# Involution kernel: matrices evicted in runs of three elements, and full-width matmuls in place of 32-column tiles

## The chip, the cores and the metric

The kernel runs on one core of a Trainium2 chip. The metric is the device time of one execution in microseconds (us); lower is better. The engines are named as in the profile: PE is TensorE (PEld its weight loads), DVE is VectorE, ACT is ScalarE, POOL is GpSimd and SP is SyncE, which here only issues DMAs.

## What is computed

The input is x, 8 x 256 x 56 x 56, float32. Two residual layers follow each other, each on a group-normalised copy of x:

```python
x = x + involution(gn(x))          # layer 0
x = x + tri_conv_block(gn(x))      # layer 1: two 3x3 convolutions with ternary weights, batch norms, ReLUs

def involution(x):                 # 7x7, 16 groups of 16 channels
    ker = einsum('bchw,oc->bohw', x, w_reduce) + b_reduce     # 256 -> 64 channels
    ker = einsum('bchw,oc->bohw', ker, w_span) + b_span       # 64 -> 49 * 16
    patches = [padded x shifted by (i, j) for i in range(7) for j in range(7)]
    return (ker.reshape(B, 16, 1, 49, H, W) * patches.reshape(B, 16, 16, 49, H, W)).sum(axis=3)
```

Every pixel has its own 7 x 7 kernel for each of the 16 groups. Only layer 0 is touched by the change.

## The kernel before

The program has three stages: the involution (`ph1`), the two convolutions (`ph2`, `ph3`, matmuls on line 202) and a last pass that combines and stores. The involution takes roughly the first half of the time.

**Tiling of the involution.** A tile is 3 x 8 pixels (`PY` x `PX`, `NP` = 24). There are 19 rows of 7 tiles (`TY`, `TX`, together `NT` = 133). The 9 x 14 neighbourhood of a tile has `NQ` = 126 positions. For one tile and one group the involution is a matrix product: the neighbourhood's pixels (126 positions by channels) against a matrix of 126 positions by 24 output pixels that holds the kernels at the places where they apply. The work goes over 16 chunks: 8 batches, and in each two halves `t` of 128 channels (8 groups).

**`prep(b)`** is a generator with ten steps, one for each strip of six image rows. POOL normalises the strip (`xn`, L304), PE reduces it to 64 channels twice over (`pk`, L310), ACT adds the bias and writes it sorted by pixel within the tile (`kr`, L323). PE also transposes the strip (`pt`, L328), ACT copies it to `stg` (L333), and a DMA on ACT's queue stores it in `xt_d` (L336; `xtd` in the profile), a padded copy in DRAM with pixels first and channels inside, one row being `WQ` pixels. There are two such copies, used by even and odd batches in turn. The strips for batch b+1 are prepared while the second half of batch b is applied.

**`generate(b, t, a)`** makes the matrices of a chunk, `a`, in 32 units. A unit is three pixels and two groups: six float32 matmuls of 64 rows, 126 columns and 133 tiles, each of which shows as two instructions (`pg`, L373). The two groups use the two halves of the PE rows and write to two banks of one PSUM tile. The eviction adds the span bias and writes to `a`, whose rows hold, for each tile, 8 groups x 24 pixels: three units of four are evicted by one DVE instruction (L385), the fourth by six ACT instructions (L381). On DVE the innermost run goes over the 133 tiles, so that one element follows another at a step of 192 elements.

**`apply_rows(b, t, a, q, i)`** applies two rows of tiles (one in the last of ten groups). For every tile there are four matmuls, one for each pair of groups, each with 32 channels as stationary columns and 48 moving columns, on the four 32-column parts of PE (`pa`, L398). The result has, for each channel, the values of both groups of its pair. One ACT instruction copies the even group's values times 1 or 0 (L406), one DVE instruction for each row adds the odd group's times 0 or 1 (L408), and POOL adds the sum to x in place (L413).

**`load_q`** fetches the neighbourhoods `q` of a group of two rows from `xt_d`: nine DMAs a row, of 14 partitions each, on the SP queue (L359). `qpool` has three buffers, and `prefetch` keeps up to three groups under way across chunks. PSUM is one pool of four tiles of two banks (`ps_tile`), shared by all of these.

**The order** is that of the loop at the end of the function: for each chunk, `generate`, then ten times apply, prefetch and one `prep` step, then the group-norm statistics of the result and its store (`x1d`). A scheduler places the instructions on the queues and sets the semaphores; each engine takes its queue in order.

Of the kernel before, what the change touches and what calls it, by code (L numbers as in the profile page):

```python
# [7 lines left out]
F32 = mybir.dt.float32  # L8
F32R = mybir.dt.float32r
AF = mybir.ActivationFunctionType  # L10
ALU = mybir.AluOpType
# [4 lines left out]
P = 128  # L16
B, C, H, W = 8, 256, 56, 56
HW = H * W
CT = C // P
K, PAD, G = 7, 3, 16  # L20
KK = K * K
GT = G // CT
GP = GT // 2
# [4 lines left out]
PY, PX = 3, 8  # L28
TY, TX = 19, W // PX
NT = TY * TX  # L30
NP = PY * PX
QY, QX = PY + K - 1, PX + K - 1
NQ = QY * QX
LEAD = (PY - 1) * QX + PX - 1
WL = LEAD + NQ
HQ, WQ = TY * PY + K - 1, 64
SR = 6
NS = -(-H // SR)
QG = 2
NQG = -(-TY // QG)  # L40
NX = PY * W
# [10 lines left out]
def involution_tri_block_kernel(  # L52
# [3 lines left out]
    nc = tc.nc  # L56
    x = x.rearrange("b c h w -> b c (h w)")
# [189 lines left out]
    with ExitStack() as ph1:  # L247
        ps_p = ph1.enter_context(tc.tile_pool(name="ps_p", bufs=4, space=PSUM))

        def ps_tile(name):  # L250
            return ps_p.tile([P, 2, 512], F32, tag="ps", name=name)
# [6 lines left out]
        work = ph1.enter_context(tc.tile_pool(name="work", bufs=2))  # L258
# [11 lines left out]
        xs = {(0, t): load_x(0, t) for t in range(CT)}  # L270
# [8 lines left out]
        half_sb = fixed([P, 2], "half_sb", half)  # L279
# [6 lines left out]
        wl = fixed([P, CT, GP, WL], "wl", w_line)  # L286
# [11 lines left out]
        def prep(b, pr):  # L298

            for s in range(NS):  # L300
                n = min(SR, H - s * SR)
                strip = xn[s % 2]
                for t in range(CT):
                    nc.gpsimd.tensor_scalar(  # L304
                        strip[:, t, :n, PAD:PAD + W],
                        xs[b, t][:, s * SR * W:(s * SR + n) * W].rearrange("p (h w) -> p h w", w=W),
                        pr[t][:, 0:1], pr[t][:, 1:2], ALU.mult, ALU.add)
                pk = ps_flat(f"pk_{b}_{s}")
                for t in range(CT):
                    nc.tensor.matmul(pk[:, :n * W], wr[:, t, :], strip[:, t, :n, PAD:PAD + W],  # L310
                                     start=(t == 0), stop=(t == CT - 1))
                ty = s * SR // PY
                for y in range(min(PY, n)):
                    m = -(-(n - y) // PY)
                    rows = pk[:, y * W:y * W + W]
                    if m == 2:
                        rows = pk[:, :n * W].rearrange("p (a f) -> p a f", f=NX)[:, :, y * W:y * W + W]
                        src = rows.rearrange("p a (t x) -> p a t x", x=PX)
                        dst = kr[:, y, :, ty:ty + m, :].rearrange("p x a t -> p a t x")
                    else:  # L320
                        src = rows.rearrange("p (t x) -> p t x", x=PX)
                        dst = kr[:, y, :, ty, :].rearrange("p x t -> p t x")
                    nc.scalar.activation(dst, src, AF.Identity, bias=br)  # L323
                nb = n // 2
                pt = ps_flat(f"pt_{b}_{s}")
                for k in range(nb):
                    for t in range(CT):
                        nc.tensor.transpose(  # L328
                            pt[:2 * WQ, k * C + t * P:k * C + (t + 1) * P],
                            strip[:, t, 2 * k:2 * k + 2, :].rearrange("p r w -> p (r w)"),  # L330
                            ident_sb)
                stg = work.tile([P, SR // 2, C], F32, tag="stg", bufs=3, name=f"stg_{b}_{s}")
                nc.scalar.copy(stg[:2 * WQ, :nb, :].rearrange("p k c -> p (k c)"),  # L333
                               pt[:2 * WQ, :nb * C])
                o = (PAD + s * SR) * WQ
                nc.scalar.dma_start(  # L336
                    xt_d[b % 2][o:o + n * WQ, :].rearrange("(k p) c -> p k c", p=2 * WQ),
                    stg[:2 * WQ, :nb, :])
                yield
# [22 lines left out]
        def generate(b, t, a):  # L362

            av = a[:NQ].rearrange("q t (g p) -> q g p t", g=GT)
            for u in range(GP * NP // 3):
                gp, p0 = u // (NP // 3), u % (NP // 3) * 3
                ps = ps_tile(f"pg_{b}_{t}_{u}")
                for j in range(3):
                    py, px = (p0 + j) // PX, (p0 + j) % PX
                    o = LEAD - py * QX - px  # L370
                    for h in range(2):
                        rows = slice(h * CR, (h + 1) * CR)
                        nc.tensor.matmul(  # L373
                            ps[:NQ, h, j * NT:(j + 1) * NT], wl[rows, t, gp, o:o + NQ],
                            kr[rows, py, px].rearrange("r a t -> r (a t)"),
                            start=True, stop=True)
                g0 = 2 * gp
                if u % 4 == 3:
                    for h in range(2):
                        for j in range(3):  # L380
                            nc.scalar.activation(  # L381
                                av[:, g0 + h, p0 + j], ps[:NQ, h, j * NT:(j + 1) * NT],
                                AF.Identity, bias=bt[:, t, g0 + h, p0 + j:p0 + j + 1])
                else:
                    nc.vector.tensor_tensor(  # L385
                        av[:, g0:g0 + 2, p0:p0 + 3],
                        ps[:NQ, :, :3 * NT].rearrange("q h (p t) -> q h p t", t=NT),
                        bt[:, t, g0:g0 + 2, p0:p0 + 3].unsqueeze(3).to_broadcast([NQ, 2, 3, NT]),
                        ALU.add)

        def apply_rows(b, t, a, q, i):

            ty, n = i * QG, min(QG, TY - i * QG)
            ps = ps_tile(f"pa_{b}_{t}_{i}")
            for r in range(n):
                for k in range(TX):
                    for g in range(GP):
                        nc.tensor.matmul(  # L398
                            ps[g * 32:(g + 1) * 32, r, k * 2 * NP:(k + 1) * 2 * NP],
                            q[:NQ, r, k, g * 32:(g + 1) * 32],  # L400
                            a[:NQ, (ty + r) * TX + k, g * 2 * NP:(g + 1) * 2 * NP],
                            start=True, stop=True)
            even, odd = (ps[:, :n, :TX * 2 * NP].rearrange("c r (k h p) -> c r k h p", k=TX, h=2)
                         [:, :, :, h].rearrange("c r k p -> c r k p") for h in range(2))
            inv = work.tile([P, QG, TX, NP], F32, tag="inv", bufs=3, name=f"inv_{b}_{t}_{i}")
            nc.scalar.activation(inv[:, :n], even, AF.Copy, scale=half_sb[:, 0:1])  # L406
            for r in range(n):
                nc.vector.scalar_tensor_tensor(inv[:, r], odd[:, r], half_sb[:, 1:2], inv[:, r],  # L408
                                               ALU.mult, ALU.add)
                m = min(PY, H - (ty + r) * PY)  # L410
                xv = xs[b, t][:, (ty + r) * NX:(ty + r) * NX + m * W]
                xv = xv.rearrange("p (y t x) -> p y t x", t=TX, x=PX)
                nc.gpsimd.tensor_tensor(  # L413
                    xv, xv, inv[:, r].rearrange("p t (y x) -> p y t x", y=PY)[:, :m], ALU.add)

        chunks = [(b, t) for b in range(B) for t in range(CT)]
        queue = [(b, t, i) for b, t in chunks for i in range(NQG)]
# [2 lines left out]
        def prefetch(upto):  # L420
            while queue and len(loads) < upto:
                k = queue.pop(0)
                loads[k] = load_q(*k)

        nprm = [None] * CT
        for b, t in chunks:
            more = b + 1 < B
            if t == 0:
                prefetch(3)
                if more:  # L430
                    xs[b + 1, 0] = load_x(b + 1, 0)
            a = apool.tile([P, NT, GT * NP], F32, tag="a", name=f"a_{b}_{t}")
            generate(b, t, a)
            steps = iter(())
            if t == 1 and more:
                xs[b + 1, 1] = load_x(b + 1, 1)
                nprm[1] = params(b + 1, 1, xs[b + 1, 1])
                steps = prep(b + 1, list(nprm))
            for i in range(NQG):
                apply_rows(b, t, a, loads.pop((b, t, i)), i)  # L440
                if t == 0 or i + 3 < NQG:
                    prefetch(3)
                if i == 4 and t == 0 and more:
                    nprm[0] = params(b + 1, 0, xs[b + 1, 0])
                next(steps, None)
            for _ in steps:
                pass
            group_norm_params(xs[b, t], ps_flat, gn2[:, b, t, :], f"b{b}{t}")
            nc.sync.dma_start(x1_d[b][t], xs[b, t])
# [131 lines left out]
```

## Time and profile before

| | |
|---|---|
| Median of 3 runs | 3955.49 us (3952.43 to 3955.94) |
| Profiled execution | 3955.94 us, its span 3954.2 us |
| PE busy, PEld busy | 2750.0 us (70%), 2414.5 us (61%) |
| DVE, ACT, POOL busy | 1253.3 us (32%), 848.0 us (21%), 302.5 us (8%) |
| DMA | 431.79 MB, 387086 packets |
| Mean granted TensorE clock | 0.825 |

Busy times are shares of the whole span and hide that the stages have different limits; so the involution has to be read by stretches. In a group line the number after x is how often the instruction ran, then come the total busy time in us and the mean of one in ns, then the idle time of the engine just before them and what ended it. The granted clock of PE is given as a share of full speed. A line of the chain in time gives the start in us, the length in us and the engine or DMA that held the end up.

### The profile page before, as it was taken

How to read it: one execution, taken by the hardware profiler on the slowest of the kernel's cores; microseconds unless marked ns; L12 is line 12 of the kernel's file. 1: busy time of each engine (PE TensorE's matmuls, PEld its weight loads, DVE VectorE, ACT ScalarE, POOL GpSimd, SP SyncE). 2: the span in 40 equal slices, each digit the busy share in tenths (PEclk: the TensorE clock that was granted, in tenths of full speed). 3: DMA queues.
4: the chain of work that ended last, by engine and by line, in shares of the span. 5: the costliest groups of instructions: out<-in, count | busy, mean ns of one | idle time of the engine just before them, and what ended most of it. 6: DMA issues, size and time to landing. Idle time of an engine off the chain costs nothing.

```text
span 3954.2 us, 73934 instructions
## 1 busy us (share of the span) xinstructions
PE 2750.0 (70%) x32132; PEld 2414.5 (61%) x32132; DVE 1253.3 (32%) x1675; ACT 848.0 (21%) x1595; POOL 302.5 (8%) x491
## 2 busy tenths in 40 slices
PE   3455565556545455554399999999799999999500
PEld 2444544445444445444288888888688888888400
DVE  5445534254452444534331111110111111110254
ACT  2122221222212122221031111110121111110243
POOL 1111111201002110110300000000200000000000
PEclk8677776667767787776599999999899999999755
DMA  5233343333334333333431111100221111100499
GB/s 182 76 120 119 120 126 115 101 117 121 116 113 124 109 118 118 122 112 105 144 128 63 63 63 63 63 31 31 79 81 63 63 63 63 63 31 0 173 406 396
DMA packets 387086, 431.79 MB, mean 109 GB/s; under 512 B 46576, under 2 KB 369742, under 8 KB 369870
## 3 DMA queue, kind: packets, MB, share of 16 engines
q1 hardware_dynamic: 350496, 360.54, 27.0%
q10 hardware_dynamic: 36268, 66.53, 4.6%
q8 instruction: 256, 4.19, 0.5%
q14 instruction: 66, 0.52, 0.0%
HBM read 295.56 MB, written 131.33 MB: 108 GB/s over the span
## 4 chain that ended last, share of the span: by engine, by line
PE 50%; DVE 17%; SPq 15%; DMA 13%; issue 3%; ACT 2%; POOL 0%; ACTq 0%; DVEq 0%; POOLq 0%
PE c L202 43%; SPq L359 15%; DVE a L385 13%; DMA xtd<-stg 3%; DMA q<-xtd 3%; PE pa L398 3%; PE pk L310 3%; DMA x1f<-x1d 2%; DMA y1f<-y1d 1%; PE pt L328 1%; ACT stg L333 1%; DVE x1f L522 1%; DMA out_y<-x1f 1%; DVE st_a L113 1%; DMA y2f<-y2d 1%
## 5 line engine op out<-in xcount | busy, mean ns | idle before, releaser
L202 PE MATMUL c<-o,wq 128*128 128x448 f32 x8064 | 1704.3, 374 | 35.2 <-ACT o L192 31.9
L202 PEld LDWEIGHTS c<-o,wq 128*128 128x128 f32 x8064 | 1525.1, 189 | 214.1 <-ACT o L192 32.4
L398 PE MATMUL pa<-a,q 126*32 126x48 f32 x17024 | 351.2, 254 | 671.8 <-DMA q<-xtd 630.3
L398 PEld LDWEIGHTS pa<-a,q 126*32 126x32 f32 x17024 | 307.3, 145 | 718.0 <-issue 497.2
L385 DVE TENSOR_TENSOR a<-pg,bt 126x798 f32<-126x798 f32 x384 | 528.3, 1524 | 7.6 <-DMA wqd<-wq_w 7.0
L373 PE MATMUL pg<-kr,wl 64*126 64x133 f32 x6144 | 442.6, 296 | 98.0 <-DVE a L385 97.3
L373 PEld LDWEIGHTS pg<-kr,wl 64*126 64x126 f32 x6144 | 399.3, 199 | 138.3 <-DVE a L385 137.5
L408 DVE SCALAR_TENSOR_TENSOR inv<-pa,half_sb,inv 128x168 f32<-128x168 f32 x304 | 105.9, 388 | 916.3 <-ACT inv L406 916.3
L381 ACT ACTIVATE a<-pg,bt 126x133 f32<-126x133 f32 x768 | 230.4, 479 | 328.7 <-PE pg L373 307.3
L465 DVE BATCH_NORM_STATS2 st<-y 128x6 f32<-128x448 f32 x112 | 70.2, 627 | 681.4 <-ACT y L464 681.4
L413 POOL TENSOR_TENSOR x<-x,inv 128x168 f32<-128x168 f32 (+1 forms) x304 | 155.5, 531 | 1026.0 <-DVE inv L408 1025.9
L406 ACT ACTIVATE inv<-pa,half_sb 128x336 f32<-128x336 f32 (+1 forms) x160 | 84.2, 526 | 610.9 <-PE pa L398 572.8
L464 ACT COPY y<-c 128x448 f32<-128x448 f32 x112 | 59.5, 532 | 663.3 <-PE c L202 663.3
L498 DVE BATCH_NORM_STATS2 st<-y 128x6 f32<-128x448 f32 x84 | 52.5, 626 | 460.9 <-ACT y L497 460.9
L310 PE MATMUL pk<-xn,wr 128*128 128x336 f32 (+1 forms) x320 | 159.7, 641 | 24.6 <-POOL xn L304 24.6
L323 ACT ACTIVATE kr<-pk,br 128x112 f32<-128x112 f32 (+1 forms) x232 | 74.6, 453 | 381.2 <-PE pk L310 380.4
L497 ACT COPY y<-c 128x448 f32<-128x448 f32 x84 | 44.7, 532 | 475.2 <-PE c L202 475.2
L304 POOL TENSOR_SCALAR xn<-x,gn 128x336 f32<-128x336 f32 (+1 forms) x160 | 95.6, 607 | 661.9 <-DVE gn L129 362.8
L310 PEld LDWEIGHTS pk<-xn,wr 128*128 128x128 f32 x320 | 77.9, 276 | 57.1 <-POOL xn L304 25.4
L221 POOL MEMSET o<- 128x3364 f32 x16 | 45.6, 2902 | 850.4 <-PE c L202 850.3
L328 PEld LDWEIGHTS pt<-ident_sb,xn 128*128 128x128 f32 x448 | 73.3, 181 | 29.1 <-issue 21.0
L113 DVE BATCH_NORM_STATS2 st_b<-x 128x6 f32<-128x448 f32 x112 | 69.8, 623 | 66.9 <-POOL x L413 66.9
(93 smaller groups left out, 965.2 us busy)
## 6 DMA issues: line engine op xcount, KB each, us to landing
q<-xtd SPq DMA_DIRECT2D x2736, 49.0 KB
xtd<-stg ACTq DMA_DIRECT2D x72, 384.0 KB
x<-in_x SPq DMA_DIRECT2D x16, 1568.0 KB
x1d<-x SPq DMA_DIRECT2D x16, 1568.0 KB
x1l<-x1d SPq DMA_DIRECT2D x16, 1568.0 KB
y1d<-y SPq DMA_DIRECT2D x112, 224.0 KB
y1l<-y1d SPq DMA_DIRECT2D x16, 1568.0 KB
y1f<-y1d SPq DMA_DIRECT2D x16, 1568.0 KB
```

The costliest lines, as they stand in the source:

```text
L113: nc.vector.bn_stats(st[:, j, :], xt[:, j * NC:(j + 1) * NC])
L202: nc.tensor.matmul(ps[:, :NC], wq[:, t, tap, t_out * P:(t_out + 1) * P], part[t][:, j * CRW + dy:j * CRW + dy + CRW, dx:dx + W], start=(n ...
L304: nc.gpsimd.tensor_scalar(strip[:, t, :n, PAD:PAD + W], xs[b, t][:, s * SR * W:(s * SR + n) * W].rearrange("p (h w) -> p h w", w=W), pr[t] ...
L310: nc.tensor.matmul(pk[:, :n * W], wr[:, t, :], strip[:, t, :n, PAD:PAD + W], start=(t == 0), stop=(t == CT - 1))
L328: nc.tensor.transpose(pt[:2 * WQ, k * C + t * P:k * C + (t + 1) * P], strip[:, t, 2 * k:2 * k + 2, :].rearrange("p r w -> p (r w)"), ident_sb)
L359: nc.sync.dma_start(q[qy * QX:(qy + 1) * QX, r], src)
L373: nc.tensor.matmul(ps[:NQ, h, j * NT:(j + 1) * NT], wl[rows, t, gp, o:o + NQ], kr[rows, py, px].rearrange("r a t -> r (a t)"), start=True, ...
L381: nc.scalar.activation(av[:, g0 + h, p0 + j], ps[:NQ, h, j * NT:(j + 1) * NT], AF.Identity, bias=bt[:, t, g0 + h, p0 + j:p0 + j + 1])
L385: nc.vector.tensor_tensor(av[:, g0:g0 + 2, p0:p0 + 3], ps[:NQ, :, :3 * NT].rearrange("q h (p t) -> q h p t", t=NT), bt[:, t, g0:g0 + 2, p0 ...
L398: nc.tensor.matmul(ps[g * 32:(g + 1) * 32, r, k * 2 * NP:(k + 1) * 2 * NP], q[:NQ, r, k, g * 32:(g + 1) * 32], a[:NQ, (ty + r) * TX + k, g ...
L408: nc.vector.scalar_tensor_tensor(inv[:, r], odd[:, r], half_sb[:, 1:2], inv[:, r], ALU.mult, ALU.add)
L413: nc.gpsimd.tensor_tensor(xv, xv, inv[:, r].rearrange("p t (y x) -> p y t x", y=PY)[:, :m], ALU.add)
```

## The change

The change has five parts.

1. In `generate`, the matmuls of the units that DVE evicts write every third column of their PSUM bank, so that the three pixels of a unit lie side by side for each tile. The DVE instruction then goes over tiles outside and pixels inside and writes three neighbouring elements at a time. ACT's units are as before.
2. `apply_rows` becomes `apply_row`. One row of tiles is applied at a time, with one matmul of 128 stationary columns and 192 moving columns for each tile, in two PSUM tiles of four and three image tiles. Each output channel then has the values of all eight groups, and for each 32 partitions one ACT and one DVE instruction pick the two groups that belong there: eight ACT and eight DVE instructions a row, on 32 partitions each. The POOL addition is as before.
3. A row of `xt_d` has 62 pixels in place of 64, so that a transposed pair of image rows has 124 partitions in place of 128, and the pad-row stores have 62.
4. The store from `stg` to `xt_d` is issued by SP in place of ACT, and `stg` has two buffers in place of three.
5. The loop goes over 19 rows in place of ten groups; prefetch still follows every second row, and `prep` still takes ten steps in a chunk.

```diff
-HQ, WQ = TY * PY + K - 1, 64
+HQ, WQ = TY * PY + K - 1, W + K - 1
...
-                stg = work.tile([P, SR // 2, C], F32, tag="stg", bufs=3, name=f"stg_{b}_{s}")
+                stg = work.tile([P, SR // 2, C], F32, tag="stg", name=f"stg_{b}_{s}")
...
-                nc.scalar.dma_start(
+                nc.sync.dma_start(
                     xt_d[b % 2][o:o + n * WQ, :].rearrange("(k p) c -> p k c", p=2 * WQ),
                     stg[:2 * WQ, :nb, :])
...
+                on_act = u % 4 == 3
...
+                        if on_act:
+                            dst = ps[:NQ, h, j * NT:(j + 1) * NT]
+                        else:
+                            dst = ps[:NQ, h, j:3 * NT:3]
                         nc.tensor.matmul(
-                            ps[:NQ, h, j * NT:(j + 1) * NT], wl[rows, t, gp, o:o + NQ],
+                            dst, wl[rows, t, gp, o:o + NQ],
...
                     nc.vector.tensor_tensor(
-                        av[:, g0:g0 + 2, p0:p0 + 3],
-                        ps[:NQ, :, :3 * NT].rearrange("q h (p t) -> q h p t", t=NT),
-                        bt[:, t, g0:g0 + 2, p0:p0 + 3].unsqueeze(3).to_broadcast([NQ, 2, 3, NT]),
+                        av[:, g0:g0 + 2, p0:p0 + 3].rearrange("q g p t -> q g t p"),
+                        ps[:NQ, :, :3 * NT].rearrange("q h (t p) -> q h t p", p=3),
+                        bt[:, t, g0:g0 + 2, p0:p0 + 3].unsqueeze(2).to_broadcast([NQ, 2, NT, 3]),
                         ALU.add)
...
-        def apply_rows(b, t, a, q, i):
...
+        def apply_row(b, t, a, q, ty):
+            inv = work.tile([P, TX, NP], F32, tag="inv", bufs=3, name=f"inv_{b}_{t}_{ty}")
+            for t0, n in ((0, 4), (4, 3)):
+                ps = ps_tile(f"pa_{b}_{t}_{ty}_{t0}").rearrange("p a (k f) -> p (a k) f", k=2)
+                for i in range(n):
+                    nc.tensor.matmul(ps[:, i, :GT * NP], q[:NQ, ty % QG, t0 + i, :],
+                                     a[:NQ, ty * TX + t0 + i, :], start=True, stop=True)
+                for j in range(4):
+                    rows = slice(j * 32, (j + 1) * 32)
+                    dst = inv[rows, t0:t0 + n, :]
+                    even, odd = (ps[rows, :n, g * NP:(g + 1) * NP] for g in (2 * j, 2 * j + 1))
+                    nc.scalar.activation(dst, even, AF.Copy, scale=half_sb[rows, 0:1])
+                    nc.vector.scalar_tensor_tensor(dst, odd, half_sb[rows, 1:2], dst,
+                                                   ALU.mult, ALU.add)
...
-            for i in range(NQG):
-                apply_rows(b, t, a, loads.pop((b, t, i)), i)
-                if t == 0 or i + 3 < NQG:
-                    prefetch(3)
-                if i == 4 and t == 0 and more:
+            for ty in range(TY):
+                i = ty // QG
+                apply_row(b, t, a, loads[b, t, i], ty)
+                if ty % QG == QG - 1 or ty == TY - 1:
+                    del loads[b, t, i]
+                    if t == 0 or i + 3 < NQG:
+                        prefetch(3)
+                if ty == 8 and t == 0 and more:
                     nprm[0] = params(b + 1, 0, xs[b + 1, 0])
-                next(steps, None)
+                if ty % 2 == 1 or ty > 16:
+                    next(steps, None)
```

More of the change, by code (lines that the diff above doesn't have):

```diff
@@ L377, in generate @@
                 g0 = 2 * gp
-                if u % 4 == 3:
+                if on_act:
                     for h in range(2):
@@ L389, in generate @@
                         ALU.add)
-        def apply_rows(b, t, a, q, i):
[L393 to L414, printed above, removed]
@@ new lines, in apply_row @@
+        def apply_row(b, t, a, q, ty):
[12 more added lines that the diff above has]
+                                                   ALU.mult, ALU.add)
+            n = min(PY, H - ty * PY)
+            xv = xs[b, t][:, ty * NX:ty * NX + n * W].rearrange("p (y t x) -> p y t x", t=TX, x=PX)
+            nc.gpsimd.tensor_tensor(
+                xv, xv, inv.rearrange("p t (y x) -> p y t x", y=PY)[:, :n], ALU.add)
```

## The prediction

> **What bounds the kernel now.** I read the page's forty slices first, then the groups, then stretches of one batch, then the SyncE queue's own waits and the chain in time. The slices split the span in two: up to about 1960 us PE is half busy at a changing clock (the involution stage), after that PE shows 9 (the convolutions) and the end is DMA. The diff touches only the first part. Its groups:
>
> ```profile
> L385 DVE TENSOR_TENSOR a<-pg,bt 126x798 f32<-126x798 f32 x384 | 528.3, 1524 | 7.6 <-DMA wqd<-wq_w 7.0
> L373 PE MATMUL pg<-kr,wl 64*126 64x133 f32 x6144 | 442.6, 296 | 98.0 <-DVE a L385 97.3
> L398 PE MATMUL pa<-a,q 126*32 126x48 f32 x17024 | 351.2, 254 | 671.8 <-DMA q<-xtd 630.3
> L408 DVE SCALAR_TENSOR_TENSOR inv<-pa,half_sb,inv 128x168 f32<-128x168 f32 x304 | 105.9, 388 | 916.3 <-ACT inv L406 916.3
> L381 ACT ACTIVATE a<-pg,bt 126x133 f32<-126x133 f32 x768 | 230.4, 479 | 328.7 <-PE pg L373 307.3
> ```
>
> In `generate` DVE never waits (7.6 us in all) and PE waits for DVE; in the apply stage PE waits for the `q` loads. Busy time by stretch: a generate, an apply of a first channel half (t=0), an apply of a second half with `prep` of the next batch in it (t=1):
>
> ```profile
> core 0: us, PE busy (x) PEld busy (x) DVE busy (x) ACT busy (x) POOL busy (x), PEclk, DMA share, GB/s
> 325.00:358.00 33.00, 26.63 (x388) 23.64 (x384) 32.93 (x28) 14.42 (x48) 0.00 (x0) 0.96 0.44 133
> 358.60:421.00 62.40, 21.36 (x1000) 18.75 (x1000) 15.49 (x44) 5.06 (x10) 10.53 (x20) 0.58 0.35 98
> 468.00:559.00 91.00, 50.55 (x1162) 38.63 (x1162) 12.11 (x35) 21.32 (x50) 20.42 (x37) 0.67 0.36 108
> ```
>
> Generate: 24 DVE evictions fill 33.0 us, 1.374 us each. What PE alone needs shows where it runs unhindered, in the same table for `pg` alone:
>
> ```profile
> 327.50:328.90 1.40, 1.40 (x28) 1.40 (x28) 1.40 (x2) 0.43 (x2) 1.00 0.18 44
> ```
>
> 28 matmul instructions in 1.40 us; their records start in pairs 110 ns apart at full clock, so a unit (12 instructions) takes 0.66 us and 32 units 21.1 us. Apply at t=0 is SyncE issuing: 122 `q` DMAs 0.436 us apart, with seven long ones, 62 us. Apply at t=1 is a loop, seen in the SyncE queue's waits and in the chain in time:
>
> ```profile
> SPq L359 <- PE pa L398: 262.1, 16, 28.5
> SPq L359 <- DMA xtd<-stg: 240.0, 64, 12.4
> ```
> ```profile
> 499.10 2.52 DMA xtd<-stg
> 501.64 0.31 SPq L359
> ...
> 503.73 1.88 DMA q<-xtd
> 505.61 1.33 PE pa L398 x56
> 506.94 2.54 PE pk L310 x4
> 509.48 1.29 PE pt L328 x6
> 510.80 0.81 ACT stg L333
> 511.62 2.53 DMA xtd<-stg
> ```
>
> The records show eight DMA semaphores used in turn over both queues, so a `q` load waits until the DMA eight places before it has landed; when that is the `stg` store, the loop turns once in 12.5 us.
>
> **What the Trainium skill says.** (1) "SBUF — State Buffer", Specifications (TRN2): two hits on a 16-byte line are needed for full bandwidth. The trace agrees that scattered writes cost: DVE's contiguous rows (168 elements 388 ns, 3136 elements 3428 ns) give 216 ns + 1.02 ns each, so 798 would take 1033 ns, and L385, writing single elements 768 bytes apart, takes 1524. (2) "PSUM — Partial Sum Buffer", Specifications (TRN2): any non-contiguous pattern slows matmuls significantly, without a figure. No matmul here writes a stepped output. (3) "DMA: Bandwidth & Descriptors", Why a DMA increments its semaphore by 16 and not by 1: a DMA is spread over the largest number of engines up to 16 that divides the slowest dimension. The packet records agree: the 126-row load of `bt` never has more than 14 packets in flight, the 128-row `stg` store 16 and more. (4) "PSUM — Partial Sum Buffer", PSUM bank collisions: two engines must not touch one bank in the same 32 partitions together; other quadrants may. No run here shows it.
>
> **The change, part by part.**
>
> *Generate.* DVE writes runs of three. At 12-byte runs, two of three DVE units start so that one element of each run stands alone on a 16-byte line: 798 x 2/3 x 1/3 = 177 elements, at the scattered surcharge (1524-1033)/798 = 0.62 ns, 0.11 us. So 1033+110 = 1143 ns; consecutive evictions overlap 150 ns today (1524-1374), giving 0.99 us, 23.8 us for 24. PE's 21.1 us and ACT's 14.4 lie below. With the two now so close and four PSUM buffers I take 26: **-7 us** a generate, 16 times, -112. Bounds: 21.2 us of DVE with no lone element (-10 us); no gain at all if the run length is not what costs. PE's stepped write is the unknown: between nothing and twice the time for the three units of four that use it. I take nothing: a convolution instruction writes 448 columns in 211 ns (1704.3 us over 8064), 0.47 ns a column, while a `pg` instruction needs 110 ns for 133, 0.83 ns each, so the write side should have slack. That is an inference, and the first rival is its failure.
>
> *Apply, t=0.* 17024 32-column matmuls go, 4256 of 192 columns come. `pk` instructions of 336 columns start 0.56 us apart at a clock of 0.5, so 192 columns take 0.32 there and 0.16 at a clock of 1.0: a row (14) 2.2 to 4.5 us against 1.35. SyncE needs 4.6 us a row (18 x 0.436 + 1.2 of long ones, halved) and covers it, except for the two ends of a chunk: the first group is released later (+1.8) and the last row comes later (+1.8). ACT: 8 small activations a row; contiguous ACT rows (540 ns for 336, 400 for 168) give 260 + 0.83 each, 340 and 320 ns, overlapping to some 0.15; 1.2 us a row. DVE: 8 at 216 + 1.02 each, 314 and 290 ns, 1.75 us a row overlapped. Both hide under 4.6; only the last half row shows, +0.4. **+4 us** a chunk; nine chunks without `prep` (+36).
>
> *Apply, t=1.* The `stg` store goes to SyncE and has 124 rows. 124 divides by 4, so four engines carry 93 packets of 1 KB each; such packets take 47 ns here, so 4.4 us instead of 1.3, landing 5.7 us after issue instead of 2.5 (estimate from the skill's rule). Behind the store stand the `q` loads: seven go on in 3.5 us, the eighth waits 2.2. The store itself should not wait for ACT: it is written after a load that SyncE needs 9 us to issue. So a group is 9.0 + 0.4 + 2.2 = 11.6 us against 12.5, seven times: -6. Against that: +4 at the ends as above, and with two `stg` buffers the copy of the last strips waits for a store of 5.7 us, with the evictions behind it on ACT, +4. **+2 us**, seven times (+14). Bounds: 10 to 13 us a group, -10 to +11.
>
> *Start.* The 14 pad-row stores have 62 rows, so two engines at 31 x 46 ns: 20 us in sequence on ACT's queue, where they now take 12, with the `w1` loads behind them; batch 0's ten stores take 4.4 us each where the strips follow each other in 2.1 now. This lies beside the weight reduction but not wholly. **+20** (10 to 30).
>
> *Nothing:* fewer transposed rows and smaller pads, hidden on PE and POOL; the POOL adds keep their number.
>
> Sum: -112 + 36 + 14 + 20 = -42. The profiled execution took 3955.94 us (span 3954.2), the median of three 3955.49, so 3914 either way.
>
> **Rivals.**
>
> *PE becomes the bound of generate* (slower). If the stepped write halves PE's pace, a pair takes 220 ns: 24 units of 1.32 and 8 of 0.66 make 37.0 us, +4 a generate, 64 + 70 = +134, 4090. It decides from 1.5 times on: 24 x 0.99 + 5.3 = 29 us leaves -4, which the other 70 eat. For it: the skill's sentence. Against: the slower stream. Between them, at 1.4 times, -72 + 70: 3954.
>
> *Runs of three do not help DVE* (the change doesn't do what it says): only the +70 remains, 4026. For it: no DVE row here has such runs. Against: `kr` written by ACT (532-byte steps, 460 ns for 112 elements) is as dear as `a`, and contiguous rows are not.
>
> *The small evictions become the bound.* If the four quadrants of a bank are read one after another by ACT and DVE in turn, a row is 8 steps of ACT, DVE and two hand-overs of 35 ns, 4 x 0.72 + 4 x 0.69 = 5.6 us, above SyncE's 4.6, and nothing runs ahead: 107 us for 19 rows at t=0 (+45), about the same at t=1 with `prep`'s 2.2 us a group on ACT. 16 x 41 on top of the sum: near 4570. Against: the two half rows lie in different banks and can alternate.
>
> **How the numbers follow.** Main case 0.42, with its own range 3850 to 3960; PE at 1.4 times 0.13; PE at twice 0.23; DVE not helped 0.10; evictions 0.12. I call no change what lies within 0.2%, 8 us. Faster: 0.33 of the main case and 0.05 of the middle one, 0.38; same 0.08; slower 0.54, though no single slower case is as likely as the main one. The range 3840 to 4110 leaves out the eviction case and a few hundredths at either end.
>
> **What would show it.** Right: L385 near 1140 ns; generate 24 to 27 us; matmul pairs of `pg` at 110 ns; t=0 apply 65 to 67 us with SyncE issuing throughout; `xtd<-stg` landing after more than 5 us and SyncE waiting about 2 us behind it. Wrong: pairs of 150 ns or more; L385 above 1400; PE waiting for ACT or DVE instead of `q`, or SyncE standing long before a store whose copy is not done.

## The result and the profile after

The changed kernel takes **4091.48 us** (median, 4089.27 to 4096.95) against 3954.76 us for the kernel before on the same chip: a ratio of 1.0349, 95% interval 1.0331 to 1.0366. It is slower by 3.5%; the forecast was 3914 us, and the time lies near the upper end of its range. The profiled execution has a span of 4087.1 us. Its groups on the page answer to those shown of before:

```profile
L402 PE MATMUL pa<-a,q 126*128 126x192 f32 x4256 | 877.1, 367 | 295.5 <-issue 126.3
L409 DVE SCALAR_TENSOR_TENSOR inv<-pa,half_sb,inv 32x72 f32<-32x72 f32 (+1 forms) x2432 | 732.6, 301 | 572.6 <-ACT inv L408 482.9
L408 ACT ACTIVATE inv<-pa,half_sb 32x72 f32<-32x72 f32 (+1 forms) x2432 | 784.6, 323 | 423.1 <-DVE inv L409 265.9
L379 PE MATMUL pg<-kr,wl 64*126 64x133 f32 x6144 | 404.0, 293 | 21.6 <-DVE a L391 20.0
L391 DVE TENSOR_TENSOR a<-pg,bt 126x798 f32<-126x798 f32 x384 | 370.6, 1042 | 22.5 <-PE pg L379 14.2
```

The `generate` eviction fell from 1524 to 1042 ns, and PE's wait for it from 97.3 to 20.0 us. In the apply stage PE waited for `q` before; now ACT and DVE name each other as the engine that ends most of their idle time. The stretches that answer to the three of before are a generate, an apply at t=0 and an apply at t=1:

```profile
core 0: us, PE busy (x) PEld busy (x) DVE busy (x) ACT busy (x) POOL busy (x), PEclk, DMA share, GB/s
613.20:637.80 24.60, 22.77 (x372) 22.20 (x368) 23.04 (x25) 14.42 (x48) 0.00 (x0) 0.97 0.39 111
637.80:713.30 75.50, 54.84 (x270) 50.53 (x270) 51.88 (x166) 45.60 (x143) 10.40 (x19) 0.89 0.40 119
754.60:857.00 102.40, 73.07 (x358) 62.92 (x358) 48.50 (x159) 63.26 (x180) 20.43 (x36) 0.90 0.31 85
```

Generate went from 33.0 to 24.6 us, the t=0 apply from 62.4 to 75.5. The wait that sets the end of a t=0 row can be read from the chain in time there:

```profile
694.77 0.34 ACT inv L408
695.11 0.03 issue
695.13 0.32 DVE inv L409
695.47 0.34 ACT inv L408
695.82 0.03 issue
695.84 0.32 DVE inv L409
696.19 0.34 ACT inv L408
696.53 0.03 issue
696.55 0.33 DVE inv L409
```

ACT and DVE take turns, 0.71 us for a pair, although the two engines work on different 32 partitions and only the DVE instruction needs the ACT one of its own 32 partitions (a quadrant). The two half rows alternate on both engines: while DVE has a quadrant of one, ACT has a quadrant of the other. So a row takes five such pairs, 3.5 us, and not eight. At t=1 the same chain passes through the store (the length on the DMA line is from issue to landing):

```profile
812.15 0.39 SPq L359
812.54 0.05 issue
812.63 8.71 DMA xtd<-stg
821.46 0.78 issue
822.24 0.34 ACT inv L408
```

What waits for the store there is ACT's next copy to `stg`, because one of the two buffers has to come free; the line of the page has such waits at 131.0 us in all:

```profile
L333 ACT COPY stg<-pt 124x768 f32<-124x768 f32 x80 | 61.4, 768 | 132.2 <-DMA xtd<-stg 131.0
```

Adding up the two traces by stage, with the stage's borders at the first eviction of `generate` on DVE and its last on either engine, the next chunk's first eviction, and the first convolution matmul:

| stage | before, us | after, us | change | forecast |
|---|---|---|---|---|
| start, to the first `generate` eviction on DVE | 90.0 | 109.8 | +19.8 | +20 |
| 16 generates | 528.9 | 402.1 | -126.8 | -112 |
| 8 applies at t=0, to the next generate | 559.6 | 678.1 | +118.5 | +32 |
| last apply (no `prep`), to the first convolution | 96.6 | 104.2 | +7.6 | +4 |
| 7 applies at t=1 with `prep`, to the next generate | 709.0 | 823.6 | +114.6 | +14 |
| sum: first convolution matmul | 1984.0 | 2117.8 | +133.8 | -42 |

After the first convolution the two are alike (1970.2 and 1969.3 us to the end of the span).

### The profile page after: what moved, and what is told of

Its sections match the earlier page's. It is cut to its first block, busy times and chain, and to the rows that moved or that the text cites. A ratio compares the mean times of both kernels' runs of the same rounds, so it can differ in the third digit from the quotient of the medians.

```text
span 4087.1 us, 53613 instructions
## 1 busy us (share of the span) xinstructions
PE 3178.9 (78%) x19364; PEld 2862.7 (70%) x19364; DVE 1726.1 (42%) x3803; ACT 1566.2 (38%) x3867; POOL 306.4 (7%) x491
## 4 chain that ended last, share of the span: by engine, by line
PE 54%; DVE 14%; DMA 14%; ACT 10%; issue 4%; SPq 3%; POOL 1%; ACTq 1%; DVEq 0%; POOLq 0%
PE c L202 42%; DMA xtd<-stg 8%; ACT inv L408 7%; DVE inv L409 7%; PE pg L379 6%; PE pa L402 5%; DVE a L391 3%; SPq L359 3%; DMA x1f<-x1d 2%; DMA y1f<-y1d 1%; ACT kr L323 1%; DVE st_b L113 1%; DVE st_a L113 1%; DVE x1f L526 1%; DMA out_y<-x1f 1%
## 5 line engine op out<-in xcount | busy, mean ns | idle before, releaser
L402 PE MATMUL pa<-a,q 126*128 126x192 f32 x4256 | 877.1, 367 | 295.5 <-issue 126.3
L402 PEld LDWEIGHTS pa<-a,q 126*128 126x128 f32 x4256 | 803.3, 216 | 360.8 <-issue 229.1
L409 DVE SCALAR_TENSOR_TENSOR inv<-pa,half_sb,inv 32x72 f32<-32x72 f32 (+1 forms) x2432 | 732.6, 301 | 572.6 <-ACT inv L408 482.9
L408 ACT ACTIVATE inv<-pa,half_sb 32x72 f32<-32x72 f32 (+1 forms) x2432 | 784.6, 323 | 423.1 <-DVE inv L409 265.9
L379 PE MATMUL pg<-kr,wl 64*126 64x133 f32 x6144 | 404.0, 293 | 21.6 <-DVE a L391 20.0
L379 PEld LDWEIGHTS pg<-kr,wl 64*126 64x126 f32 x6144 | 394.0, 200 | 28.7 <-DVE a L391 20.2
L391 DVE TENSOR_TENSOR a<-pg,bt 126x798 f32<-126x798 f32 x384 | 370.6, 1042 | 22.5 <-PE pg L379 14.2
L328 PEld LDWEIGHTS pt<-ident_sb,xn 128*124 128x124 f32 x448 | 54.3, 150 | 110.7 <-ACT stg L333 88.0
L328 PE MATMUL pt<-ident_sb,xn 128*124 128x128 f32 x448 | 71.8, 299 | 76.1 <-ACT stg L333 70.4
L310 PE MATMUL pk<-xn,wr 128*128 128x336 f32 (+1 forms) x320 | 106.7, 456 | 27.6 <-POOL xn L304 27.5
L333 ACT COPY stg<-pt 124x768 f32<-124x768 f32 x80 | 61.4, 768 | 132.2 <-DMA xtd<-stg 131.0
```

The costliest lines, as they stand in the source:

```text
L328: nc.tensor.transpose(pt[:2 * WQ, k * C + t * P:k * C + (t + 1) * P], strip[:, t, 2 * k:2 * k + 2, :].rearrange("p r w -> p (r w)"), ident_sb)
L379: nc.tensor.matmul(dst, wl[rows, t, gp, o:o + NQ], kr[rows, py, px].rearrange("r a t -> r (a t)"), start=True, stop=True)
L391: nc.vector.tensor_tensor(av[:, g0:g0 + 2, p0:p0 + 3].rearrange("q g p t -> q g t p"), ps[:NQ, :, :3 * NT].rearrange("q h (t p) -> q h t p ...
L402: nc.tensor.matmul(ps[:, i, :GT * NP], q[:NQ, ty % QG, t0 + i, :], a[:NQ, ty * TX + t0 + i, :], start=True, stop=True)
L408: nc.scalar.activation(dst, even, AF.Copy, scale=half_sb[rows, 0:1])
L409: nc.vector.scalar_tensor_tensor(dst, odd, half_sb[rows, 1:2], dst, ALU.mult, ALU.add)
```

## The experiments

**Theory A**: two waits eat the gain. In the new apply, ACT and DVE take turns within one PSUM tile, at every t; and the store of 124 rows runs over few DMA engines and holds the SyncE queue at t=1. **Rivals**: the full-width matmuls on PE are the bound (C); the many small evictions are the cost, not their turns; the store on SyncE is the cost, not its rows. Every ratio is against the kernel before, timed on the same chip; its medians beside these kernels were 3951.97, 3954.66 and 3956.61 us, so a difference of less than some 5 us between two of them says nothing.

### One part at a time, on the kernel before

*The interleaving alone* (parts of `generate` as in the change's diff, nothing else).

> The kernel before, with the interleaved kernel matrices alone (the stepped PSUM output and the eviction in runs of three); the apply stage, the row length and the store stay as before. Theory A (alternating small evictions): the generate part is worth all of its 127 us, since the apply stage of before waits for q loads on SyncE's queue and is not touched: 3955 - 127 = 3828 us, generate at about 25 us a chunk, apply at 62.4 us (t=0) and as before at t=1. Theory B (loads only move: a shorter generate gives the q loads less time to run ahead, so the apply pays back a part): with 3 groups loaded ahead at most, at most one group of 9 us a chunk comes back, 3828 to 3955 us. Theory C (full-width matmuls are what is dear): says the same as A here.

Measured: 3863.41 us, ratio 0.978 (0.9764 to 0.9797). The generates give the whole 126.5 us, and 30 us come back at t=1, where the first `pa` matmul now starts 10.3 us after the generate in place of 5.9. The direction of theory B was right, its cause not. The chain of this kernel at such a place:

```profile
200.83 7.06 DMA x1d<-x
207.93 6.36 DMA x<-in_x
214.31 3.80 DVE st_a L113 x7
218.13 0.36 DVE mv_a L115
218.49 0.14 issue
218.63 0.57 PE gnp_a L117 x2
```

It is not a `q` load: the store of the chunk's result, the load of the next batch's `x` and its statistics on DVE come next, and PE's queue stands behind the statistics' small matmuls. That was hidden by the longer generate.

*The rows and the store alone.*

```diff
-HQ, WQ = TY * PY + K - 1, 64
+HQ, WQ = TY * PY + K - 1, W + K - 1
-                stg = work.tile([P, SR // 2, C], F32, tag="stg", bufs=3, ...)
+                stg = work.tile([P, SR // 2, C], F32, tag="stg", ...)
-                nc.scalar.dma_start(
+                nc.sync.dma_start(
```

> The kernel before, with the transposed row of 62 pixels, the stg store on SyncE and two stg buffers; generate and apply as before. Theory A: the start costs +20 us; the t=1 chunks lose about 0.9 us a group (13.4 for 12.5, 7 groups and 7 chunks: +44 us), the last store of a chunk some 3 us more before the next (+20): 4020 to 4050 us in all. Theory of the prediction (store lands after 5.7 us and a group takes 11.6 us): +20 at the start, -6 us a t=1 chunk, +4 with two buffers, 3955 + 20 - 14 = 3960 us. If the stores explain nothing of the loss beyond the start: 3975 us.

Measured: 4053.17 us, ratio 1.0249 (1.0229 to 1.0269), 3 us above theory A's span. The start costs 18.4 us; a t=1 chunk, generate and gap with it, 6.4 to 15.0 us more. The median time between two `stg` stores within a t=1 chunk, from their issue times, the second to the sixth gap of each chunk, is 13.5 us against 12.1 before. The forecast's 11.6 us a group is refuted without the new apply having any part in it.

*The store on SyncE alone* (the last line pair of that diff; 64 pixels a row and three buffers stay).

> The kernel before with one edit: the stg store is issued by SyncE instead of ACT (128 rows, three buffers kept). If a q load waits at t=1 for the store because the store, issued from ACT's queue, takes its place among the eight DMA semaphores late (the loop of 12.5 us a group), the store after the loads of a group turns that into SyncE's own pace of 9.0 + 0.4 us a group: -3 us x 7 groups x 7 chunks = -150, 3805 us; at least half of it if the transposes or params hold some groups. If the loop is held by the ACT copy or PE's transposes and not by the place of the store, nothing moves: 3952 us, or some 20 us more for the added issues on SyncE.

Measured: 3818.85 us, ratio 0.9653 (0.9635 to 0.967), with 9.7 us between stores. So moving the store is a gain of 136 us, and the loop of 12.5 us in the kernel before was made by the store's place. What SyncE waits for shows it: before it stood 240.0 us for `xtd<-stg`, now that line is gone from its list, and the store itself waits little for its copy:

```profile
SPq L359 <- PE pa L398: 254.3, 18, 25.0
SPq L336 <- ACT stg L333: 31.2, 11, 11.6
```

*The rows, with three buffers* (the kernel of "the rows and the store alone" with `bufs=3` back).

> The kernel before with rows of 62 pixels and the store on SyncE, but with the three stg buffers kept (in place of two). Two buffers measured 4053 us. If the wait of ACT for a free stg buffer (359 us in that kernel) is what holds the groups: 10 to 50 us less. If SyncE's stand behind a store that lands late holds them, the third buffer changes nothing: 4045 to 4055 us.

Measured: 4032.4 us, ratio 1.0192 (1.0174 to 1.021). The third buffer is worth some 21 us in this kernel, so the buffers are no main cause here; in the changed kernel, where ACT waits for a free one, a third was not tried. Against the store on SyncE alone, this kernel differs in the row length only: 62 pixels in place of 64 cost 214 us, of which 13 lie in the start.

*The new apply alone* (`apply_row` and its loop in the kernel before).

> The kernel before, with the full-width apply and its 8 small evictions a half row alone; generate, row length, store and buffers as before. Theory A (the evictions of one half row go in turns between ACT and DVE, and set 4.8 to 5.6 us a row against 4.6 of SyncE, with 8 us for a chunk's first row): 8 t=0 chunks and one more at +14.8 us, +133; at t=1 the store loop of 12.5 us a group covers the rows, but the first row and the last evictions show, +4 to +10 us in 7 chunks: 3955 + 133 + 28..70 = 4116 to 4158 us. The prediction's value for this part (+4 us a chunk, 16 chunks): 4019 us. Theory C (full-width matmuls on PE): the same total, but PE busy without gaps in the t=0 chunks instead of waiting for DVE.

Measured: 4264.99 us, ratio 1.0787 (1.0771 to 1.0803), 107 us above the top of what theory A said. The t=0 chunks came nearly as it said (119.2 us for 103.0 in the median, generate and gap with them). The t=1 chunks did not: 160.7 for 134.4 us. SyncE's waits and the chain tell why:

```profile
SPq L359 <- DMA xtd<-stg: 394.5, 72, 12.1
```
```profile
837.18 0.31 ACT inv L402
837.52 0.36 ACT kr L323
838.03 0.21 issue
838.24 0.31 ACT inv L402
838.58 0.81 ACT stg L333
839.40 3.09 DMA xtd<-stg
842.51 0.31 SPq L359
842.86 0.39 SPq L359
```

The `stg` copy and the store stand in ACT's queue between the evictions that take turns with DVE, so the loop of before is closed through ACT, and 14.5 us lie between stores. In the whole change this doesn't happen, because the store is on SyncE there: the parts' effects do not add (-88, +101 and +313 would make +326, and the change costs 137).

### Undoing one cause in the changed kernel

*Rows of 64 pixels again* (`WQ = 64`; store on SyncE and two buffers stay).

> The changed kernel with rows of 64 pixels again, so that the stores have 128 rows and use all DMA engines; the store stays on SyncE with two buffers. Theory A: -20 us at the start; the store lands after about 2.5 us instead of 8.6, so SyncE no longer stands behind it (2.3 to 3.1 us a group) and a t=1 group falls from 13.4 us to the rows' own 10.5 to 11: -2.5 us x 7 groups x 7 chunks = -120, with the tail of each chunk -3 us: 4091 - 20 - 120..145 = 3925 to 3950 us. If the evictions set the t=1 groups too, little but the start goes: 4060 to 4075 us. Theory C (PE): also 4060 to 4075 us.

Measured: 3963.2 us, ratio 1.0026 (1.0018 to 1.0035). It gives 128 us: 20 in the start and 101.5 at t=1, where 9.3 us lie between stores. That is 13 us short of theory A's span, but 97 us from what its rivals said; PE, buffers and evictions are those of the changed kernel.

*Evictions of a half row in two passes.*

```diff
                 for j in range(4):
                     rows = slice(j * 32, (j + 1) * 32)
-                    dst = inv[rows, t0:t0 + n, :]
...
                     nc.scalar.activation(...)
+                for j in range(4):
+                    rows = slice(j * 32, (j + 1) * 32)
                     nc.vector.scalar_tensor_tensor(...)
```

> The changed kernel with the evictions of a half row in two passes: first ACT's four quadrants, then DVE's four, in place of ACT and DVE by turns. Same instructions, same count, same result. Theory A (by turns within one PSUM tile, each instruction waits for the one before on the other engine): a row costs at most 2.8 us on ACT (8 x 0.34) and 2.6 on DVE, both below SyncE's 4.6, so the t=0 chunks fall from 75.5 to 65 to 68 us and their ends by 2 to 4 us; t=1 moves by 0 to -5 us a chunk, since the few-engine store stays: 4091 - 9 x 10 - 0..35 = 3965 to 4010 us. Theory C (192-column matmuls on PE set the rows, 5.1 us of PE at the low clock): 4085 to 4091 us. Theory of small instructions (the number of evictions, not their turns): 4085 to 4091 us.

Measured: 3996.17 us, ratio 1.0101 (1.0085 to 1.0116), so 95 us less than the changed kernel with the same instructions, in the same number and of the same mean duration. Its waits, and its stretches at t=0 and t=1 (columns as in the table of stretches above):

```profile
DVE inv L411 <- ACT inv L406: 424.1, 203, 6.9
ACT inv L406 <- PE pa L402: 185.8, 131, 5.6
```
```profile
616.60:682.40 65.80, 51.54 (x270) 47.63 (x270) 52.16 (x167) 47.57 (x148) 10.40 (x19) 0.92 0.44 128
721.50:821.00 99.50, 74.65 (x358) 64.73 (x359) 48.53 (x159) 61.33 (x180) 20.41 (x36) 0.88 0.32 87
```

ACT waits for PE, no longer for DVE, and the t=0 apply is 65.8 us, the forecast's "65 to 67 us". ACT and DVE are as busy in those 65.8 us as in the 75.5 of the changed kernel, and PE's matmuls are the same too. That speaks against the rival of the small evictions' number, and against PE as the bound at t=0. At t=1 it gives 3 us in seven chunks: there something else ends last.

*Half of the moving columns* (this kernel leaves out half of the products).

```diff
-                    nc.tensor.matmul(ps[:, i, :GT * NP], ..., a[:NQ, ty * TX + t0 + i, :], ...)
+                    nc.tensor.matmul(ps[:, i, :GT * NP // 2], ..., a[:NQ, ty * TX + t0 + i, :GT * NP // 2], ...)
-                    even, odd = (... for g in (2 * j, 2 * j + 1))
+                    even, odd = (... for g in (2 * (j % 2), 2 * (j % 2) + 1))
```

> The changed kernel with 96 of the 192 moving columns in each matmul of the apply (half of the products are left out; the evictions keep their number, size and turns, quadrants 2 and 3 reading the columns of 0 and 1). Theory C (PE): its matmul time of 2.9 us a row, 877 us in all, halves, and the t=0 chunks fall to SyncE's 63 to 66 us: about 4091 - 9 x 10 = 4000 us or less. Theory A (turns of ACT and DVE): PE waits for DVE longer instead; a chunk loses only the shorter first and last half row, 0.5 to 1.5 us: 4065 to 4085 us.

Measured: 4062.71 us, ratio 1.0268 (1.0253 to 1.0283): 29 us less, 2 us beyond theory A's span and 63 from theory C's. A t=0 chunk falls by 2.2 us. The turns stay:

```profile
L402 PE MATMUL pa<-a,q 126*128 126x96 f32 x4256 | 846.1, 383 | 217.4 <-issue 105.1
ACT inv L408 <- DVE inv L409: 252.4, 513, 5.2
```

The first line is from the page, the second from the waits. PE shows 846.1 us busy with half the columns against 877.1 with all, so the records of a PE that is held up from behind cannot be read as its need.

*An output tile of ACT's own.*

```diff
+            ev = work.tile([P, TX, NP], F32, tag="ev", bufs=3, ...)
...
-                    nc.scalar.activation(dst, even, AF.Copy, scale=half_sb[rows, 0:1])
-                    nc.vector.scalar_tensor_tensor(dst, odd, half_sb[rows, 1:2], dst,
+                    nc.scalar.activation(ev[rows, t0:t0 + n, :], even, AF.Copy, scale=half_sb[rows, 0:1])
+                    nc.vector.scalar_tensor_tensor(dst, odd, half_sb[rows, 1:2], ev[rows, t0:t0 + n, :],
...
```

> The changed kernel with an SBUF tile of its own for ACT's product: ACT writes ev, DVE reads ev and writes inv. Same instructions and turns in the program's order. If ACT waits for DVE because both write one SBUF tile, the turns go and the time falls as with two passes, to about 4000 us. If the wait comes from both reading one PSUM tile, nothing moves: 4085 to 4095 us, with ACT still waiting some 270 us for DVE.

Measured: 4087.63 us, ratio 1.0332 (1.0317 to 1.0347), no change, and the wait is still there:

```profile
ACT ev L409 <- DVE inv L410: 263.9, 462, 4.2
```

That both engines write one SBUF tile is not the reason. Two tiles of data are left that both of them touch: the PSUM tile, which both read, and `ev`, which ACT writes and DVE reads. No run separates these two. Against `ev` speaks that the nine loads of a `q` row write different partitions of one SBUF tile 0.436 us apart, each landing after some 1.9 us, so writers of different partitions don't wait for each other there; this is an argument, and not a run that takes one of the two away. "PSUM — Partial Sum Buffer" in the Trainium skill (PSUM bank collisions raise a hardware error) lets two engines use one bank in different 32 partitions; here the wait stands between different 32 partitions all the same, as a semaphore in the program. Whether the chip would need it wasn't tried.

### Both cures, and the best version

*Two passes and rows of 64 pixels.*

> The changed kernel with both cures: evictions of a half row in two passes, and rows of 64 pixels so that the store has 128 rows. If the turns of ACT and DVE and the store over few engines are separate causes, their gains add: two passes gave 4091 - 3996 = 95 us, long rows 4091 - 3963 = 128 us, so 3868 us, below the kernel before. If at t=1 both stand behind one loop, the second cure helps t=1 more once the first is in (rows of 2.7 us in place of 4 to 5): down to 3820 us. Above 3900 us they were partly one cause.

Measured: 3776.76 us, ratio 0.9545 (0.953 to 0.9559), 43 us below the lowest value expected. The four kernels make a square (7 applies at t=1 with their gaps, from the traces):

| | rows of 62 | rows of 64 |
|---|---|---|
| in turns | 823.6 | 722.1 |
| two passes | 820.5 | 623.7 |

Two passes give 3 us with the short rows and 98 with the long ones. This is how two causes look that lie behind each other: the store's 13.4 us a group covers the turns, and with it gone the turns show. The SyncE waits for the store tell how, of the kernel with long rows and turns (first line) and with two passes (second line):

```profile
SPq L336 <- ACT inv L408: 178.7, 63, 9.9
```
```profile
SPq L336 <- ACT stg L333: 87.4, 32, 11.2
```

The engine named in the first line misleads. In both kernels a store that SyncE waits for starts 0.03 us after its own copy has ended; the eviction named had ended by the time the store was issued. So both wait for the copy, which stands in ACT's queue between the evictions: 185 us in all with the turns, 87 with two passes.

*The interleaving and the store on SyncE*, with the old apply, three buffers and rows of 64 pixels.

> The kernel before with two edits: the interleaved kernel matrices and the stg store on SyncE (128 rows, three buffers); apply as before. Theory A: the gain of the interleaving alone (-88 us measured) plus that of the store on SyncE, 3863 - 150 = 3713 us, and up to 30 us less still, since the 4 us a t=1 chunk that the q loads took back with interleaving alone come from the same loop. If the store's place is worth nothing: 3863 us.

Measured: **3735.48 us**, ratio 0.9446 (0.9429 to 0.9464): the fastest of all, 219 us below the kernel before. -88 and -136 add up to -224, so these two parts hardly touch each other; the value expected, 3713 us, was 22 us too low, 14 of them because it put the store at -150. The changed kernel with both cures stays 41 us behind this one, which keeps the old apply. (The two differ in the number of `stg` buffers too, but in the trace of the kernel with both cures no copy waits for one.)

## Why the prediction failed, point by point

**Right, in part by luck.** The start: +20 forecast, +19.8 measured, and gone in the kernel with 64-pixel rows. But the text judged 20 out of 10 to 30, and it did not count the two buffers, with which some 5 us of it go (18.4 us with rows and store alone, 13.8 with a third buffer). Generate: -7 us forecast, -7.9 measured. Its evictions follow each other 1.00 us apart where 0.99 was said, by two errors that cancel: they take 1042 ns in the mean and not 1143, but they overlap less, and DVE now waits 22.5 us in all. The surcharge for the element of a run that stands alone is real and half as large as forecast. Split by unit, the records of L391 show it: the units whose runs start at a multiple of 16 bytes in `a` take 988 ns, the two of three whose runs cross such a border 1068 and 1071 (984 to 988 and 1066 to 1077 in four more of these kernels). That is 80 ns for 266 elements, for which the text's 0.62 ns make 165. PE's stepped write was taken at nothing, and L379 went from 296 to 293 ns, its pairs still 110 ns apart; the rival that gave PE half its pace, the largest one, is refuted, and so is the one in which runs of three don't help. The store was said to land after more than 5 us with SyncE waiting about 2 us behind it; both happen. One sum of the text is not the one that its terms give: PE at 1.4 times makes 24 x 0.92 + 5.3 = 27.5 us, so -88 in all where it has -72; no conclusion hangs on it.

**The step that failed at t=0** is "Both hide under 4.6; only the last half row shows, +0.4". It priced the evictions of each engine by itself, 1.2 us a row on ACT and 1.75 on DVE, each overlapping the one before. The single instructions were right (323 and 301 ns in the mean), the overlap was not: with two passes they follow each other without a gap but don't overlap, so eight take 2.6 and 2.4 us. And in the change they go in turns: rows come mostly 3.5 to 4.8 us apart, 3.94 in the mean of a chunk's last nine. Nor does SyncE's 4.6 us a row cover that: three groups of `q` are loaded ahead, and the kernel before ran through those first rows at once. Measured: +14.8 us a chunk for +4. Some of it seems to come from work that was hidden before: the last t=0 chunk, which has no next batch to load and take statistics of, grew by 8.8 us (70.2 to 79.0), the others, where DVE's statistics stand between the evictions, by 12.6 to 16.9. No run took the statistics out. With two passes the excess is +4.8 (597.8 for 559.6 us in eight chunks), so the forecast's +4 was about right for evictions that don't wait for each other.

**The steps that failed at t=1** are the landing of the store, the group built on it, and a term that was missing. The packets' 4.4 us were right only without other traffic: at the start of the changed kernel, where few `q` packets run, a store that went out alone had its packets done in 4.3 to 5.4 us. At t=1 some 900 `q` packets run beside it, one of its packets takes 66 ns in place of 47, and the store took 8.71 us where 5.7 was said (its 372 packets alone some 7.5). A group takes 13.4 us where 11.6 was forecast with a bound of 13, so the sign of this term was wrong. Missing was the store's new place in the queue: a chunk's first store now stands behind `q` loads and goes out 20.2 us after the generate in place of 12.3 (18.8 with the store on SyncE alone). Together +16.4 us a chunk for +2: about 7.9 before the first store, 6.2 between the first and the last, 2.4 behind it. The time from the last apply matmul to the next generate grew by 5.9 us, from 6.2 to 12.1, but not through the new apply, from which the text took its +4 at the ends: with rows and store alone it is 12.2 us.

**The rivals.** The last one named the mechanism, quadrants read by ACT and DVE in turn, and gave it 0.12. Its own reading of "against", that two half rows in different banks can alternate, was right too: that makes 3.9 us a row of its 5.6. What was missing is the case between: alternating half rows that are still slower than the loads. The text saw no run for the skill's sentence on banks and left it there; a wait set by the program was not thought of. That the time lies inside the stated range is luck: the range was drawn without the eviction case, and the two terms that brought it there, +118.5 and +114.6, stood at +32 and +14.

**What was not seen**: part 4 of the change, the store on SyncE, was priced only together with its short rows. Apart it gains 136 us, and the row length takes 214 back.

## What to carry to other kernels

When two engines evict one PSUM tile, price the sequence of their instructions in program order, and try issuing all of one engine's before the other's: here the same instructions in another order gave 95 us. Look at how many packets of a DMA are under way at once before changing its number of rows: of the store with 124 rows mostly four were, of that with 128 rows mostly sixteen, and rows of 62 pixels in place of 64 moved 3% fewer bytes and cost 128 to 214 us. Where two waits lie behind each other, undoing one may show nothing; make the square of both.

## What the runs showed of the hardware that was not expected

- DVE writing 798 elements in runs of three takes 988 ns where the runs start at a multiple of 16 bytes and some 1070 where they cross such a border; the line through the contiguous rows gives 1033, and single elements 768 bytes apart take 1524. The bias that DVE reads has the same runs of three, so whether reading or writing makes the 80 ns is open.
- Matmuls that write every third PSUM column are not slower (293 for 296 ns, pairs 110 ns apart in both), against the general sentence of "PSUM — Partial Sum Buffer", Specifications (TRN2), in the Trainium skill.
- ACT on 32 partitions and 72 or 96 elements takes 323 ns in the mean; 336 elements on 128 partitions take 540. Splitting an eviction into quadrants made 84.2 us of ACT 784.6.
